# Two-layer decoder on one core: the last mixture's dense pair of groups is routed inside the second layer's attentions, its expert chunks begin at the mixture's second step, and the first set's scatters go three to a step

## The chip, the cores and the metric

The kernel runs on one core of a Trainium2 chip. The metric is the device time of one execution in microseconds (us); lower is better. Everything is float32. PE is the matmul engine (PEld its weight loads), DVE the vector engine, ACT the scalar engine, POOL the general engine that also issues the indirect DMAs, and SP the engine that issues most other DMAs.

## The reference, cut to what matters

The input is 32 sequences of 128 tokens with 128 features each (4096 tokens), and a context of the same shape. Two layers follow each other. Each has self-attention, cross-attention to the context and a mixture of 16 experts of which every token takes 4. The change is about the second layer's mixture:

```
def _swiglu(x, wg, wd, wu):
    return silu(x @ wg.T) * (x @ wu.T) @ wd.T
...
E = 16
TOP_K = 4
```

A router (a 16 x 128 weight and a bias per expert) scores each token against the 16 experts. The four best are taken, a softmax over their four scores gives their weights, and the output of the token is the weighted sum of the four experts' `_swiglu` plus one shared expert's, added to the token. The tokens are normalised ahead of each part (`_layernorm`).

## The kernel before, in words

**Groups, batches, sets.** A group `g` is 512 tokens (`GT`; 8 groups), a batch is 128 tokens (`S`; 4 batches to a group, `GB`; 32 in all, counted by `u`). A set `n` is two groups, so 8 batches (`NBR`); there are 4 sets. In the last mixture the sets 0, 2 and 3 (`SETS`) go by rows, and set 1 (groups 2 and 3) goes dense.

**By rows.** `Tables.route` (L1997) picks the four experts of each token, `Tables.placed` works out a place for each of the 4 x 1024 rows so that the rows of one expert lie together in tiles of 128 rows, and `Tables.way_out` (L2093) sends the normalised rows to these places in DRAM (`rows_in`) with indirect DMAs from POOL: for each batch `u` four of them, one for each choice `k`, 64 KB each, so 32 for a set. A set has 48 tiles, which are worked in 12 quads of four. `rows_of` (L2152) fetches a quad's rows (256 KB, L2154) and, for each tile, reads its expert from `owners` (L2159) and fetches that expert's weights (192 KB, L2162). `rows_turned` (L2170) transposes the rows (`prows`), `rows_up` and `rows_down` make the expert's matmuls (`pg`, `pu`, `pyrows`) and store the result to `rows_out` (L2193). `way_back` (L2198) gathers with 32 indirect DMAs a set, and `added` (L2209) adds the rows times their weights (`parts`) to `x`.

**Dense.** Groups 2 and 3 go through all 16 experts and the shared one, a chunk each: 17 chunks a group, 34 in all. `chunk_up` (L2212) multiplies (`pg<-hx`, `pu<-hx`) and scales the product by the expert's share (L2223), `chunk_down` accumulates into `y`. The shares are made by `route_softmax` (L1771); `send` (L1841) transposes them (`pct`, L1849) and writes them to DRAM (`combined`, L1853), and `fetched` (L2135) reads them back spread over 128 partitions, 1 MB for four experts of a group, four such a group. The shared expert alone is also needed for the other six groups (`alone`, one chunk each).

**The order of the work.** `steps` (L1188) writes the program step by step: in step `s` each stage `(stage, at, every, n)` that is due issues its instructions in the order of the list, and after each of them one piece of the stages under `between` is issued; what is left of these follows at the end of the step. Within `tc.manual_schedule` each named engine keeps exactly this order. The attentions of the second layer (`second_layers`, L2523) are one such run of steps (PE, DVE, ACT and POOL from step 8 on); the last mixture (`last_layer`, L2108) is the next, with SP's order written out too. The step numbers of the two are separate; below they are called attention steps and steps.

**What is routed where.** In the attentions, `rnorm`, `rscaled`, `rturn`, `routing`, `choose`, `placed` and `way_out` prepare set 0, whose scatters go four to an attention step from 35 on. Inside the last mixture, at its own steps, the dense set 1 is normalised (0), scaled (1), turned and routed (2), its shares chosen (3) and sent (4); set 2 is turned and routed at 4, placed at 6 and scattered from 7 on, two batches to a step; set 3 at 10, 12 and 13, one batch to a step. Quad `q` (0 to 35, set by set) is fetched at step `q` - 1 and transposed at step `q` + 1, so set 2's first quad at step 13, and set 3's at step 25. The dense chunks begin at step 6, one a step up to 23, then one every second step up to 36, and two a step after the quads. Set 3's gathers and additions come one batch a step from steps 39 and 41.

Of the kernel before, what the change touches and what calls it, by code (L numbers as in the profile page):

```python
# [9 lines left out]
F32 = mybir.dt.float32  # L10
# [945 lines left out]
def fast_decoder(ctx: ExitStack, tc: tile.TileContext, ins, spans, out: bass.AP):  # L956
# [847 lines left out]
    def mixture(tag, W, route, per, last, weights_of, kept=lambda g: None):  # L1804
# [13 lines left out]
        def turn(wk, g):  # L1818
            pool = edge if g in groups(0) else wk
            hs[g] = pool.tile([128, GT], F32, name="hx", bufs=2 if g in groups(0) else 5)  # L1820
            by_feature(xn.pop(g), hs[g])

        def routing(wk, n):
            lg = sm([128, NBR, E], "logits")
            for i, g in enumerate(groups(n)):
                for b in range(GB):
                    mm(lg[:, i * GB + b, :], lhsT=hs[g][:, bass.ts(b, S)], rhs=W["r"], start=True, stop=True)
            choices[n] = route(lg, edge)
            choose(n, 1)
# [130 lines left out]
    class Tables:  # L1960
# [32 lines left out]
        def kept(self, g):  # L1993
            self.xn[g] = self.spare[:, g]
            return self.xn[g]
# [97 lines left out]
        def way_out(self, n, u):  # L2093
            b, g = u % GB, n * NBR // GB + u // GB
            for k in range(4):
                sent = nc.gpsimd.indirect_dma_start(  # L2096
                    out=rows_in[n],
                    out_offset=bass.IndirectOffsetOnAxis(ap=self.places[n][:, k, u : u + 1], axis=0),
                    in_=self.xn[g][:, b],
                    in_offset=None,  # L2100
                )

                tc.declare_no_dep(sent.ins, group=f"rows{n}", reason="rows of different places")
                tc.add_to_no_dep_group(f"rows{n}", sent.ins)
                nc.gpsimd.nop()
                yield

    def last_layer(tag, W, stages, of_expert, tables):  # L2108
# [3 lines left out]
        send, made = stages[5], stages[-1]  # L2112
# [8 lines left out]
        def scaled(g):  # L2121
            xn[g] = wk.tile([128, GB, D], F32, name="xr", bufs=6)
            yield from normed(wk, g, *factors.pop(g), xn[g], nc.vector)

        def turn(g):
            hs[g] = wk.tile([128, GT], F32, name="hx", bufs=NG - 2)
# [11 lines left out]
        def routing(n):  # L2138
# [4 lines left out]
            choices[n] = tables.route(lg, n) if n in SETS else route_softmax(lg, edge)  # L2143
            next(choices[n])

        def chosen(n):
            comb = yield from choices.pop(n)
            if comb is not None:
                made["combs"][n] = comb
# [96 lines left out]
        for s in range(6, NQ + 1):  # L2246
            if s < 2 * QUADS or s % 2 == 0:
# [7 lines left out]
        at[s + 3], at[s + 5] = alone[4:5], alone[5:6]  # L2255
        LAST = s + 6
# [3 lines left out]
        for before, g in zip([None, *dense_groups], dense_groups):  # L2260
            for j in range(E // NS):
                fetches.append(((g, j), 5 if before is None else step_of[before, NS * j + NS - 1] + 1))
# [19 lines left out]
        def several(stage, keys):  # L2282
            def run(_):
# [5 lines left out]
        dense_n = ({1, 2, 3} - set(SETS)).pop()  # L2289
        n2, n3 = SETS[1:]  # L2290
        batches = lambda n: [(n, u) for u in range(NBR)]
        once = lambda stage, k, s: (lambda _: stage(k), s, 1, 1)
# [4 lines left out]
            (several(turn, of_set(dense_n)), 2, 1, 1),  # L2297
            once(routing, dense_n, 2),
            (lambda _: send(wk, dense_n), 4, 1, 1),
            (several(turn, of_set(n2)), 4, 1, 1),  # L2300
            once(routing, n2, 4),
            once(tables.owned, n2, 8),
            (several(turn, of_set(n3)), 10, 1, 1),
            once(routing, n3, 10),
            once(tables.owned, n3, 14),
# [7 lines left out]
                once(several(norm, of_set(dense_n)), None, 0),  # L2313
                once(several(scaled, of_set(dense_n)), None, 1),
                once(several(norm, of_set(n2)), None, 1),
                once(several(scaled, of_set(n2)), None, 2),
                once(chosen, dense_n, 3),
                once(chosen, n2, 5),
                once(several(norm, of_set(n3)), None, 5),
                once(tables.placed, n2, 6),  # L2320
                *((each(tables.way_out, batches(n2)[i::2]), 7, 1, 4) for i in range(2)),
                once(several(scaled, of_set(n3)), None, 8),
                once(chosen, n3, 11),
                once(tables.placed, n3, 12),
                (each(tables.way_out, batches(n3)), 13, 1, NBR),
# [4 lines left out]
                (each(way_back, batches(n3)), NQ + 3, 1, NBR),  # L2330
                (each(added, batches(n3)), NQ + 5, 1, NBR),
# [191 lines left out]
    def second_layers(stages, early, late, after, tables):  # L2523
# [11 lines left out]
        placed = lambda _: tables.placed(0)  # L2535

# [13 lines left out]
            (first(rturn), 20, 4, R),  # L2550
# [6 lines left out]
            (first(routing), 25, 1, 1),  # L2557
            (lambda _: tables.owned(0), 36, 1, 1),
            between=[
# [4 lines left out]
                (first(rscaled), 19, 4, R, xturn),  # L2564
                (first(rnorm), 18, 4, R),
# [3 lines left out]
                (lambda u: tables.way_out(0, u), 35, 1, NBR),  # L2569
# [39 lines left out]
    mixture0 = mixture("l0f", W0F, route_groups, 2, False, lambda c: (W0F[k][:, bass.ts(c, 128)] for k in "gud"))  # L2609
# [4 lines left out]
    with tc.tile_pool(name="l1early", bufs=1, reuse_waits="tile") as early:  # L2614
# [18 lines left out]
        mixture1 = mixture("l1f", W1F, lambda lg, _: tables.route(lg, 0), 1, True, of_expert, tables.kept)  # L2633
# [39 lines left out]
```

## Time and profile before

| | us |
|---|---|
| median of 6 runs | 1428.47 (1422.72 to 1433.62) |
| the profiled execution's own time | 1429.33 |
| its span, first to last instruction | 1427.5 |
| PE busy | 1270.2 (89%) |
| DVE busy | 856.9 (60%) |
| ACT busy | 576.9 (40%) |
| POOL busy | 533.7 (37%) |
| last mixture, 1128 to 1427: PE busy | 258.59 |
| last mixture: POOL busy | 161.47 |

The span lies 1.83 us below the profiled execution's own time; the rest lies around it. Busy shares are averages over very different stretches, so they say little about a change in one place. A line of a timeline begins with its start and its length in us, then engine, line of the kernel, operation, output and inputs; in brackets is how long the engine stood idle ahead of it, and what ended that. "issue" there means that nothing in the profile ended it. Lines with SPq, ACTq or POOLq are DMA issues.

### The profile page before, as it was taken

Reading aid. Unit: us, or ns where it says so; the run is one execution under the profiler, and the core shown is the slowest. Engines: PE = TensorE matmul, PEld = TensorE weight load, DVE = VectorE, ACT = ScalarE, POOL = GpSimd, SP = SyncE. Lnnn points to the kernel's source line nnn. Section 1 sums busy time; section 2 is a strip of 40 time slices with the busy share of each in tenths; the row PEclk is TensorE's granted clock in tenths of the full one; section 3 lists DMA queues with packets and bytes.
Section 4 is the critical chain, followed back from the end, with each engine's and each line's share of the span. In section 5 each row is a group of like instructions: output and inputs, shape, how many; then the busy total and the mean of one; then the engine's idle time right before and its main releaser. Section 6 shows DMA issues by size and latency. Waiting matters only on the chain. (4 is left out here: it accounts for less than half of the span.)

```text
span 1427.5 us, 27808 instructions
## 1 busy us (share of the span) xinstructions
PE 1270.2 (89%) x10753; PEld 848.1 (59%) x10753; DVE 856.9 (60%) x2271; ACT 576.9 (40%) x848; POOL 533.7 (37%) x729
## 2 busy tenths in 40 slices
PE   3689999999999998699999988999986779789897
PEld 2357777777777786444444455556653476567654
DVE  6646767676776684375775546756664455434564
ACT  1355445454554432223232235545534443234322
POOL 5233242535232140222000115445427416574665
PEclk7789999999999999789999999989988889999999
DMA  9501111111111112525135020000001379599943
GB/s 347 173 1 31 31 31 43 40 41 31 31 32 31 31 39 54 130 46 120 40 80 120 0 95 2 2 1 2 2 4 34 100 230 312 183 305 297 285 142 95
DMA packets 89531, 129.08 MB, mean 90 GB/s; under 512 B 9872, under 2 KB 63760, under 8 KB 87984
## 3 DMA queue, kind: packets, MB, share of 16 engines
q1 hardware_dynamic: 76624, 102.59, 25.9%
q0 software_dynamic: 6144, 12.60, 2.9%
q10 hardware_dynamic: 6624, 12.05, 2.2%
q8 instruction: 87, 1.43, 0.4%
q14 instruction: 52, 0.43, 0.1%
HBM read 99.34 MB, written 27.85 MB: 89 GB/s over the span
## 5 line engine op out<-in xcount | busy, mean ns | idle before, releaser
L1280 ACT ACTIVATE e<-scores 128x1024 f32<-128x1024 f32 x128 | 124.0, 1021 | 64.6 <-PE scores L977 64.6
L977 PE MATMUL y<-sg,wide 128*128 128x512 f32 x224 | 117.6, 613 | 7.4 <-DVE sg L2223 2.5
L977 PE MATMUL pg<-hx,wide 128*128 128x512 f32 x224 | 119.5, 616 | 0.0
L977 PE MATMUL pu<-hx,wide 128*128 128x512 f32 x224 | 118.3, 610 | 0.0
L2198 POOL DMA_INDIRECT back<-rows_out,place x96 | 92.7, 966 | 50.7 <-DVE x L2209 24.6
L1295 DVE STREAM_TRANSPOSE by_token<-sums 128x512 f32<-128x512 f32 x64 | 45.6, 713 | 101.1 <-PE sums L977 101.1
L1126 POOL TENSOR_SCALAR xn<-x,mv,r 128x128 f32<-128x128 f32 x80 | 67.5, 850 | 91.7 <-PE pxn L1135 82.8
L1097 POOL TENSOR_SCALAR r<-mv 128x4 f32<-128x4 f32 x48 | 11.5, 240 | 221.9 <-DVE mv L1116 221.5
L1531 ACT ACTIVATE e<-xscores 128x1024 f32<-128x1024 f32 x64 | 62.0, 1021 | 79.9 <-PE xscores L977 79.9
L1882 ACT ACTIVATE sg<-pg 128x512 f32<-128x512 f32 x72 | 43.0, 597 | 123.0 <-PE pg L977 115.5
L977 PE MATMUL sums<-e,v 128*32 128x128 f32 x2048 | 78.2, 297 | 16.0 <-POOL v L1075 15.4
L977 PE MATMUL scores<-qb,k 32*128 32x512 f32 x512 | 80.8, 703 | 12.9 <-ACT qb L1466 4.5
L1883 DVE TENSOR_TENSOR sg<-sg,pu 128x512 f32<-128x512 f32 x72 | 49.3, 685 | 66.6 <-PE pu L977 63.6
L977 PEld LDWEIGHTS sums<-e,v 128*32 128x32 f32 x2048 | 57.9, 118 | 47.7 <-POOL v L1075 20.8
L1097 POOL TENSOR_SCALAR r2x<-mv 128x2 f32<-128x2 f32 x16 | 3.7, 233 | 210.8 <-DVE mv L1116 210.8
L977 PEld LDWEIGHTS pu<-hx,wide 128*128 128x128 f32 x224 | 43.7, 197 | 54.2 <-issue 51.4
L2096 POOL DMA_INDIRECT rows_in<-xr,place x64 | 62.5, 976 | 34.6 <-issue 18.3
L1579 ACT COPY av<-po 128x512 f32<-128x512 f32 x64 | 37.5, 586 | 89.5 <-PE po L977 89.4
L1545 DVE COPY v<-pval 128x512 f32<-128x512 f32 x64 | 43.5, 680 | 50.1 <-PE pval L977 50.1
L977 PE MATMUL po<-e,v 128*64 128x128 f32 x1024 | 65.3, 280 | 8.5 <-DVE v L1545 8.5
L2183 DVE TENSOR_TENSOR sgrows<-sgrows,pu 128x512 f32<-128x512 f32 x36 | 24.7, 687 | 78.4 <-PE pu L977 48.3
L977 PE MATMUL po<-av,wide 128*128 128x256 f32 x256 | 63.4, 403 | 8.1 <-DVE av L1599 8.1
(300 smaller groups left out, 2920.9 us busy)
## 6 DMA issues: line engine op xcount, KB each, us to landing
row_weights<-in_w1f_dram SPq DMA_DIRECT2D x144, 192.0 KB, 3.7
factor<-factors SPq DMA_DIRECT2D x64, 256.0 KB, 4.7
share<-combined SPq DMA_DIRECT2D x32, 512.0 KB, 11.8
rows_in<-in_few SPq DMA_DIRECT2D x36, 256.0 KB, 4.2
rows<-rows_in SPq DMA_DIRECT2D x36, 256.0 KB, 4.8
rows_out<-yrows ACTq DMA_DIRECT2D x36, 256.0 KB, 3.9
share<-combined SPq DMA_DIRECT2D x8, 1024.0 KB
wide<-in_w1f_dram SPq DMA_DIRECT2D x1, 3272.0 KB
```

Source lines behind the costliest of these rows:

```text
L977: last[0] = nc.tensor.matmul(*args, **kw)
L1126: eng.tensor_scalar(n[:, b, :], x[g][:, b, :], mv[:, b, 0:1], r[:, b : b + 1], ALU.subtract, ALU.mult)
L1280: nc.scalar.activation(e[-1], ps[:, bass.ts(n, 2)].rearrange("p c i s -> p (c i) s"), AF.Exp, scale=scale)
L1295: nc.vector.transpose(tt.rearrange("p i t r -> p (i t r)"), po.rearrange("p i s -> p (i s)"))
L1531: nc.scalar.activation(e[-1], ps[:, n].rearrange("p r c s -> p (r c) s"), AF.Exp, scale=scale)
L1545: nc.vector.tensor_copy(v[:, bass.ts(n, XC), :], pv)
L1579: nc.scalar.copy(avs[w][n][:, :, bass.ts(b, S)], po)
L1882: nc.scalar.activation(sg, pg, AF.Silu)
L1883: nc.vector.tensor_tensor(sg, sg, pu, ALU.mult)
L2096: sent = nc.gpsimd.indirect_dma_start(out=rows_in[n], out_offset=bass.IndirectOffsetOnAxis(ap=self.places[n][:, k, u : u + 1], axis=0), in ...
L2183: nc.vector.tensor_tensor(sg, sg, pu, ALU.mult)
L2198: nc.gpsimd.indirect_dma_start(out=outs[n, u][:, k], out_offset=None, in_=rows_out[n], in_offset=bass.IndirectOffsetOnAxis(ap=places[n][:, ...
```

## The change

The dense set's norm, scaling, turn, routing, choosing and sending move from the mixture's steps 0 to 4 into the attention steps 26 to 43. Its turned groups are kept in the tiles of the context's first two groups (`cx[0]`, `cx[1]`), which the cross-attention has read by then. The share fetches of its first group move from step 5 to step 0. The dense chunks begin at step 1, one a step up to 19, then one every second step up to 36; six of 34 instead of nine are left for the steps after the quads. Set 2's routing moves from step 4 to 2, its placing from 6 to 4 and its scatters from 7 to 5; set 3's from 10, 12 and 13 to 6, 8 and 10. Set 0's scatters go three instead of four to an attention step, over 11 steps instead of 8, from the same step on. Set 3's gathers and additions go two batches a step, and the last step of all is 45 instead of 48. Two rings become shorter (`xr` 6 to 4 tiles, `hx` 6 to 4).

```diff
     def turn(wk, g):
-        pool = edge if g in groups(0) else wk
-        hs[g] = pool.tile([128, GT], F32, name="hx", bufs=2 if g in groups(0) else 5)
+        pool, bufs = (edge, 2) if g in groups(0) else (wk, 5)
+        hs[g] = more[g] if g in more else pool.tile([128, GT], F32, name="hx", bufs=bufs)
         by_feature(xn.pop(g), hs[g])
...
     def kept(self, g):
-        self.xn[g] = self.spare[:, g]
-        return self.xn[g]
+        if g * GB // NBR in SETS:
+            self.xn[g] = self.spare[:, g]
+        return self.xn.get(g)
...
-    def way_out(self, n, u):
-        b, g = u % GB, n * NBR // GB + u // GB
-        for k in range(4):
+    def way_out(self, n, some):
+        for u, k in some:
+            b, g = u % GB, n * NBR // GB + u // GB
...
-        for s in range(6, NQ + 1):
-            if s < 2 * QUADS or s % 2 == 0:
+        for s in range(1, NQ + 1):
+            if s < 20 or s % 2 == 0:
                 at[s] = [todo.pop(0)]
...
-        at[s + 3], at[s + 5] = alone[4:5], alone[5:6]
-        LAST = s + 6
+        at[s + 3], at[s + 4] = alone[4:5], alone[5:6]
+        LAST = s + 5
...
-                fetches.append(((g, j), 5 if before is None else step_of[before, NS * j + NS - 1] + 1))
+                fetches.append(((g, j), 0 if before is None else step_of[before, NS * j + NS - 1] + 1))
...
-            (several(turn, of_set(dense_n)), 2, 1, 1),
-            once(routing, dense_n, 2),
-            (lambda _: send(wk, dense_n), 4, 1, 1),
-            (several(turn, of_set(n2)), 4, 1, 1),
-            once(routing, n2, 4),
-            once(tables.owned, n2, 8),
-            (several(turn, of_set(n3)), 10, 1, 1),
-            once(routing, n3, 10),
-            once(tables.owned, n3, 14),
+            (several(turn, of_set(n2)), 2, 1, 1),
+            once(routing, n2, 2),
+            once(tables.owned, n2, 6),
+            (several(turn, of_set(n3)), 6, 1, 1),
+            once(routing, n3, 6),
+            once(tables.owned, n3, 12),
...
-                once(several(norm, of_set(dense_n)), None, 0),
-                once(several(scaled, of_set(dense_n)), None, 1),
-                once(several(norm, of_set(n2)), None, 1),
-                once(several(scaled, of_set(n2)), None, 2),
-                once(chosen, dense_n, 3),
-                once(chosen, n2, 5),
-                once(several(norm, of_set(n3)), None, 5),
-                once(tables.placed, n2, 6),
-                *((each(tables.way_out, batches(n2)[i::2]), 7, 1, 4) for i in range(2)),
-                once(several(scaled, of_set(n3)), None, 8),
-                once(chosen, n3, 11),
-                once(tables.placed, n3, 12),
-                (each(tables.way_out, batches(n3)), 13, 1, NBR),
+                once(several(norm, of_set(n2)), None, 0),
+                once(several(scaled, of_set(n2)), None, 1),
+                once(chosen, n2, 3),
+                once(several(norm, of_set(n3)), None, 3),
+                once(tables.placed, n2, 4),
+                (each(tables.way_out, to_send(n2, 2)), 5, 1, 4),
+                once(several(scaled, of_set(n3)), None, 5),
+                once(chosen, n3, 7),
+                once(tables.placed, n3, 8),
+                (each(tables.way_out, to_send(n3, 1)), 10, 1, NBR),
...
-                (each(way_back, batches(n3)), NQ + 3, 1, NBR),
-                (each(added, batches(n3)), NQ + 5, 1, NBR),
+                *((each(way_back, batches(n3)[i::2]), NQ + 3, 1, NBR // 2) for i in range(2)),
+                *((each(added, batches(n3)[i::2]), NQ + 5, 1, NBR // 2) for i in range(2)),
...
-            (first(rturn), 20, 4, R),
+            (first(rturn), 20, 4, 2 * R),
...
-            (first(routing), 25, 1, 1),
+            (first(routing), (25, 33), 1, 2),
             (lambda _: tables.owned(0), 36, 1, 1),
+            (lambda _: send(early, 1), 43, 1, 1),
...
-                (first(rscaled), 19, 4, R, xturn),
-                (first(rnorm), 18, 4, R),
+                (first(rscaled), 19, 4, 2 * R, xturn),
+                (first(rnorm), 18, 4, 2 * R),
...
-                (lambda u: tables.way_out(0, u), 35, 1, NBR),
+                (lambda i: tables.way_out(0, to_send[3 * i : 3 * i + 3]), 35, 1, 11),
+                (lambda _: choose(1, 3), 34, 1, 7),
...
-        mixture1 = mixture("l1f", W1F, lambda lg, _: tables.route(lg, 0), 1, True, of_expert, tables.kept)
+        route = lambda lg, n: tables.route(lg, n) if n in SETS else route_softmax(lg, edge)
+        mixture1 = mixture("l1f", W1F, route, 1, True, of_expert, {2: cx[0], 3: cx[1]}, tables.kept)
```

## The prediction

> **What bounds the kernel now.** I read the page's busy shares and chain first: PE is busy 89% of the span, so waits matter only where PE really stops. A table by stretches (columns: length, then busy us of PE, PEld, DVE, ACT, POOL, then clock, DMA share, GB/s) shows where:
>
> ```profile
> 1085.00:1100.00 15.00, 4.38 (x60) 2.98 (x60) 6.37 (x29) 2.41 (x3) 10.70 (x16) 0.75 0.10 32
> 1100.00:1128.00 28.00, 19.15 (x236) 9.61 (x230) 8.55 (x21) 13.16 (x16) 20.86 (x27) 0.80 0.12 39
> 1150.00:1172.00 22.00, 17.21 (x105) 16.16 (x105) 7.76 (x33) 8.69 (x15) 0.00 (x0) 0.77 0.60 181
> 1220.00:1230.00 10.00, 3.23 (x14) 1.92 (x13) 1.45 (x4) 1.18 (x2) 3.35 (x4) 0.79 0.33 90
> 1250.00:1275.00 25.00, 23.16 (x136) 16.68 (x136) 8.32 (x12) 9.26 (x16) 18.90 (x21) 1.00 0.95 308
> 1375.00:1400.00 25.00, 25.00 (x66) 11.61 (x65) 17.46 (x35) 5.96 (x10) 17.91 (x18) 1.00 0.20 61
> ```
>
> The granted clock falls with it. PE is starved at the end of the attentions (1085 to 1128), once near 1150 and once near 1225. After that it is full, but in the middle so is the DMA. The timelines of SP, POOL, PE and ACT then give the chain through the last mixture:
>
> ```profile
> 1124.68 0.96 POOL L2096 DMA_INDIRECT rows_in<-wide,place  x1 [0.30 <-issue]
> 1126.96 0.34 SPq L2154 DMA_DIRECT2D rows<-rows_in  x1
> 1131.87 0.66 PE L2170 MATMUL prows<-in_few,rows 128*128 128x128 f32 x4 [0.85 <-DVE x L1173]
> 1152.83 1.03 PE L1849 MATMUL pct<-in_few,comb 128*16 128x128 f32 x8 [3.94 <-DVE comb L1800]
> 1183.28 1.12 POOL L2096 DMA_INDIRECT rows_in<-xr,place  x1 [5.91 <-DVE expert_ends L2082]
> 1223.31 0.96 POOL L2096 DMA_INDIRECT rows_in<-xr,place  x1 [0.30 <-issue]
> 1225.56 0.33 SPq L2154 DMA_DIRECT2D rows<-rows_in  x1
> 1228.21 1.09 PE L2170 MATMUL prows<-in_few,rows 128*128 128x128 f32 x4 [6.77 <-DMA rows<-rows_in]
> 1298.60 0.33 SPq L2154 DMA_DIRECT2D rows<-rows_in  x1
> 1361.09 0.43 SPq L2154 DMA_DIRECT2D rows<-rows_in  x1
> 1374.00 0.33 ACTq L2193 DMA_DIRECT2D rows_out<-yrows  x1
> 1376.90 0.94 POOL L2198 DMA_INDIRECT back<-rows_out,place  x1 [3.83 <-DVE x L2209]
> 1417.00 0.94 POOL L2198 DMA_INDIRECT back<-rows_out,place  x1 [0.30 <-issue]
> ```
>
> Set 0's last scatter releases the first rows 1.3 us later; step 1 begins at 1131.87. At step 4 PE waits for the dense set's routing (1152.83). Set 2's scatters run back to back, 1183.28 to 1224.27, and PE waits 6.77 us for them at step 13. From 1298.60 to 1361.09 SP fetches 11 quads at 5.68 us each (four weight issues of together 4.3 us, the rest rows and register loads), while a step costs PE 3.11 us, or 5.69 with a chunk: SP and the DMA set the pace there. The last quad's store (1374.00) frees set 3's 32 gathers, 1376.90 to 1417.94, and they set the end.
>
> **The change, part by part.** All sums go against the profiled execution: span 1427.5, time 1429.33, which is 0.86 above the median 1428.47. I follow four marks: first rows fetch F (1126.96), step 13 (1228.21), step 36 (1365.73), end (1427.5).
>
> *Up to F: +11.5.* Three scatters a step take 11 attention steps (35 to 45) instead of 8 (35 to 42). A scatter costs POOL 1.265 us with its gap. At the end of step 39, 15 instead of 20 are out. The stall around 1087 to 1098 contains four scatters between the norm's power and the scaling; one leaves it, so all after it comes 1.27 us sooner: the range check of 1108.58 at 1107.3. From there POOL has 17 scatters (21.5), four copies of v (0.46 with gap, 1.8) and two range checks (3.0): 26.3 us, ending at 1133.6 instead of 1125.64, +8. The second check also waits for the last average, and the scatters of steps 44 and 45 stand behind it. The copies of v come sooner, so attention itself ends about 4 us earlier, but it isn't last any more.
>
> To it come the dense set's norm, turn and routing inside attention steps 26 to 40: two turns on PE (0.66 each), 16 logits (1.85), transposes for the shares (1.03), eight pairs of statistics on DVE (0.46 each), scaling (0.34 on DVE, 0.85 on POOL, four each), some 20 small routing operations (3.9 in all where they stand now). PE has between 8.4 and 10 of every 10 us busy from 985 to 1055, so the turns aren't hidden; the logits fall before the 4.1 us in which PE waits for DVE near 1055, which covers them (1.85 if that cover is gone). I take +3, between +1.3 (turns alone) and +9 (every operation in a row); nothing is removed there, so no gain. Scatters landing beside the share traffic: +0.5, at most +3.
>
> Moved past SP's queue: four share fetches of 1 MB now stand at step 0, ahead of the first rows. They wait for the combined weights sent at attention step 43, landed about 1126 plus 3, so they are issued near 1129 to 1131; 1172 to 1186, where the same fetches ran before, moved about 400 GB/s, so 4 MB take 10.5 us, done about 1141, as the rows are issued at 1138.5. Queued behind them are the rows, then all weights; PE's transposes wait for these. I charge the 2 us overlap to the next mark's slack. The Trainium skill, DMA: Bandwidth & Descriptors, Queues, rings and completion order, says each engine consumes one issuer's descriptors in ring order; it speaks against this placement, and with it the rows could not pass the shares. By the rule 2 us more, by the rows above none if the traffic is thinned by SP's own pace.
>
> *F to step 13: 101.25 to 90.75, −10.5.* The dense routing leaves steps 2 to 4, set 2's takes its place; chunks lie in steps 1 to 12 (12 instead of 7). Each step by its nearest row: F to step 2 was 9.9 (landing, transposes, weights), plus 0.86 for the chunk's down product, 10.8; step 2 (two turns, logits, chunk) like the old step 10, 8.9; step 3 5.7; step 4 with the places like the old step 12, 9.3; step 5 with their DVE chain like the old step 7, 7.4; step 6 for set 3 again 8.9; 5.8; step 8 9.3; 7.4; three of 5.75. Sum 90.75. Set 2's scatters start 2.6 before step 6, as they did before step 8: F+39.5; 32 take 41.0: F+80.5; rows 1.3 and 2.5 later, F+84.3, 6.4 us before PE wants them. So the 6.77 us wait goes, and behind it PE itself is late next. Each us of delay beyond 6.4 in that DVE chain costs a us; bounds −3 and −16.
>
> The idle before step 1 grows to some 11 us, and matmuls after a gap are slow: after the 6.77 us wait, the pair for pg took 1.91 instead of 1.02. But step 1 was slow before too (its eight pg matmuls at 1133.24 took 2.11 where later ones take 1.06), so I add 0. The Trainium skill, TensorE: Matmul & The Clock Gate, What's actually happening, has the clock halved after about 3.4 us idle and back after 3.4 us of work; by it the ceiling would be 1.7 us.
>
> *Step 13 to step 36: 137.5 to 125.3, −12.2.* Set 2's rows leave SP at F+81.8; 23 more quads at 5.6 us (5.36 over the first five, 5.68 late; nearer to the late one, as half of these steps hold a chunk and gathers run) are 128.8, two share issues 0.8, and 4.64 from last fetch to transposes: F+216. PE has 16 instead of 18 chunks here (5.2 us less), so it is not last. Bounds −5 (the chunks alone) and −18 (5.36).
>
> *Step 36 to end: +2.5.* PE's tail loses three chunks (9 to 6, 7.7 us), which buys nothing: the 41.0 us of gathers after the last store remain, and in the old profile both ended within 1 us of each other. Set 3's last additions now stand in step 44, before the last shared chunk (step 45) on DVE, so its multiply (0.70), down product (1.0) and part of the x transposes follow the last gather, +2.5; 0 if DVE were free, +4 with a cold clock.
>
> Sum +11.5 − 10.5 − 12.2 + 2.5 = −8.7: 1429.33 becomes 1420.6, less 0.86 for the median: 1419.8, say 1420.
>
> **The rivals.** *Start hardly later (0.22): 1411.* Added attention work falls into waits (POOL idles 6.1 us between 1068 and 1126, PE 10.6 between 1085 and 1100) and F moves by 3 instead of 11.5. Against it: POOL's sum above.
>
> *Pace unchanged (0.15): 1427.* At 0.95 DMA share a better order moves no more bytes; step 13 to 36 then saves only the two chunks. For it: 308 GB/s between 1250 and 1275. Against it: PE waits for rows there (2.87 and 1.98 us) with cold steps behind them, which the lead of 6.4 us at step 13 removes.
>
> *Shares first (0.10): 1437, slower.* The share buffers may lie where the attentions still work; then the head of SP's queue waits for their end and holds rows and weights back. With the upper bound of the added work the attentions end at 1141 (1131.8 + 9); four issues 1.6, 4 MB at the 286 GB/s of 1330 to 1350 14.7, rows 2.5: step 1 at 1160 instead of 1143, 17 us more. The chunks would be queued from step 1 on but wait there for their shares: the change would not do what it says. It decides if step 1's transposes start after 1158.
>
> **How the numbers follow.** The forecast has 0.53; its own range is 1412 to 1429. 0.5% is 7.1 us, about what a measurement of this kernel can tell from no change; the line is at 1421.3, so the forecast gives 0.30 to faster and 0.23 to no change. With the first rival faster has 0.52, with the second same has 0.38, slower 0.10. The range, 1406 to 1433, reaches into the first rival and past the second, and leaves out most of the third.
>
> **What would show it.** First rows fetch at 1138 (right if 1134 to 1142), the last set-0 scatter near 1136, no PE wait for comb in step 4, no wait above 2 us at step 13, set 2's scatters starting 40 us after the first rows, last store 8 to 14 us earlier, gathers still last. Wrong if rows come before 1131 (faster) or step 1 begins after 1158.

## The result, and the profile after

The changed kernel takes 1431.20 us (median of 37 executions, 1422.46 to 1446.43) and the kernel before, run beside it, 1423.92 (median of 79). The ratio is 1.0062, with a 95% interval of 1.0045 to 1.0078: slower by 0.6%, where I had forecast faster by 0.6%. The profiled execution has a span of 1433.5 us and an own time of 1435.66; the prediction's sum for it was 1420.6.

Four of the stretches that the prediction showed, in the profile after (same columns):

```profile
1085.00:1100.00 15.00, 6.91 (x99) 4.25 (x97) 11.38 (x44) 5.20 (x7) 7.83 (x12) 0.90 0.08 24
1100.00:1128.00 28.00, 19.78 (x223) 10.15 (x223) 8.55 (x21) 13.30 (x16) 22.45 (x29) 0.81 0.12 36
1150.00:1172.00 22.00, 20.41 (x132) 16.05 (x131) 11.86 (x37) 7.92 (x14) 0.00 (x0) 0.97 0.75 218
1220.00:1230.00 10.00, 9.46 (x50) 6.49 (x51) 3.53 (x6) 3.55 (x6) 7.56 (x9) 1.00 0.70 211
```

The two holes that the change was to fill are filled: PE has 20.41 of 22 us around 1160 (17.21 before) and 9.46 of 10 around 1225 (3.23). The timelines of POOL, SP and PE show what was paid for it:

```profile
1128.81 0.78 SPq L1854 DMA_DIRECT2D combined<-xn  x2
1131.77 1.97 SPq L2137 DMA_DIRECT2D share<-combined  x4
1137.28 0.95 POOL L2098 DMA_INDIRECT rows_in<-wide,place  x1 [0.30 <-issue]
1142.60 0.32 SPq L2154 DMA_DIRECT2D rows<-rows_in  x1
1146.05 1.09 PE L2170 MATMUL prows<-in_few,rows 128*128 128x128 f32 x4 [14.33 <-DMA rows<-rows_in]
1183.50 1.09 POOL L2098 DMA_INDIRECT rows_in<-xr,place  x1 [6.17 <-DVE expert_ends L2084]
1238.70 0.60 PE L2170 MATMUL prows<-in_few,rows 128*128 128x128 f32 x4
1376.49 0.33 ACTq L2193 DMA_DIRECT2D rows_out<-yrows  x1
```

PE stands idle for 14.33 us before step 1, which begins at 1146.05 instead of 1131.87. Step 13 (1238.70) no longer waits for set 2's rows. But the last store, at 1376.49, is 2.5 us later than before, not 8 to 14 earlier.

To compare executions I use marks that every kernel has. A, B and C are POOL's range checks of the attentions' results (the first instruction of each, `in_range<-rec`), counted from the end: the sixth, the fourth and the last, 980.07, 1042.90 and 1129.90 in the profile before. (One expectation below counts A and B differently; its times say which are meant.) s1, s13 and s36 are the first transposes of steps 1, 13 and 36. Of each kernel, the us between marks, on a chip of the kind on which the first result was measured:

```
                          A-B     B-C    C-s1   s1-s13  s13-s36  s36-end   A-end
before                  62.83   87.00    1.97   96.34   137.52    61.77   447.43
changed                 71.22   81.15   15.45   92.65   129.52    65.28   455.27
e10_four_again          71.22   85.94   14.44   92.12   128.86    63.94   456.52
e6_four_late            70.40   86.12    2.77   93.78   130.91    65.31   449.29
e8_chunks_to_tail       71.21   86.05    2.93   88.13   135.73    76.42   460.47
e20_all_three_third     63.59   87.88    1.90   93.75   131.86    64.60   443.58
e19_best_again          62.00   87.87    2.56  101.32   131.61    60.12   445.48
```

From A to the end the changed kernel is 7.8 us longer than the one before; the ratio of 1.0062 is 8.8 us. What lies before A is left out, since A itself lies up to 11 us apart in these executions, most of it in stretches that the edits hardly touch (last section). Each row is one execution, and executions of one kernel differ by more than the kernels do: e20_all_three_third took 1410.76 to 1435.79 us, with a median of 1427.76, and the one profiled took 1414.75. So the marks say where time goes, and the ratios how much it is. A second execution of the changed kernel (e9_after_again) repeats its row to 0.3 us.

### The profile page after: what moved, and what is told of

Its sections match the earlier page's. It is cut to its first block, busy times and chain, and to the rows that moved or that the text cites. A ratio compares the mean times of both kernels' runs of the same rounds, so it can differ in the third digit from the quotient of the medians.

```text
span 1433.5 us, 27807 instructions
## 1 busy us (share of the span) xinstructions
PE 1265.8 (88%) x10753; PEld 844.7 (59%) x10753; DVE 854.1 (60%) x2267; ACT 574.9 (40%) x846; POOL 539.0 (38%) x733
## 5 line engine op out<-in xcount | busy, mean ns | idle before, releaser
L1126 POOL TENSOR_SCALAR xn<-x,mv,r 128x128 f32<-128x128 f32 x84 | 72.2, 866 | 91.4 <-PE pxn L1135 82.7
L977 PE MATMUL scores<-qb,k 32*128 32x512 f32 x512 | 79.5, 693 | 11.1 <-ACT qb L1466 4.5
L977 PE MATMUL sums<-e,v 128*32 128x128 f32 x2048 | 75.2, 289 | 12.8 <-POOL v L1075 12.1
L977 PE MATMUL pg<-hx,wide 128*128 128x512 f32 x156 | 83.7, 619 | 0.0
L977 PE MATMUL pu<-hx,wide 128*128 128x512 f32 x156 | 81.8, 606 | 0.0
L977 PEld LDWEIGHTS y<-sg,wide 128*128 128x128 f32 x224 | 36.1, 191 | 65.5 <-DVE sg L1886 36.6
L977 PEld LDWEIGHTS xscores<-qk 64*128 64x128 f32 x1024 | 59.6, 188 | 13.8 <-issue 8.3
```

Of the source, the lines that this page charges most:

```text
L977: last[0] = nc.tensor.matmul(*args, **kw)
L1126: eng.tensor_scalar(n[:, b, :], x[g][:, b, :], mv[:, b, 0:1], r[:, b : b + 1], ALU.subtract, ALU.mult)
```

## The experiments

The chips that ran them are of two kinds: on one the kernel before takes about 1424 us, on the other 1543 to 1551. Each ratio is to the kernel before on the same chip. I call them the faster and the slower chip, but that the chip makes the difference isn't shown: of the chip numbers that the runs carry (15, 8, 2 and 11), number 8 stands at runs of both kinds. The expectations call PE TensorE, DVE VectorE, ACT ScalarE and POOL GpSimd.

**1. The spread alone, and without it.** My first theory was a late start made by the spread (as the prediction had it); the rivals were the early chunks and the shares' transfer. e1_four and e10_four_again are the same kernel on the slower and the faster chip, e2_three_only and e14_three_again another one, both on the slower.

```diff
 # e1_four, e10_four_again: the changed kernel with
-                (lambda i: tables.way_out(0, to_send[3 * i : 3 * i + 3]), 35, 1, 11),
+                (lambda i: tables.way_out(0, to_send[4 * i : 4 * i + 4]), 35, 1, NBR),
 # e2_three_only, e14_three_again: the kernel before with
-                (lambda u: tables.way_out(0, u), 35, 1, NBR),
+                (lambda i: tables.some_out(0, to_send[3 * i : 3 * i + 3]), 35, 1, 11),
```

> The changed kernel with one thing undone: the first set's 32 scatters go four to an attention step in 8 steps again (everything else as changed). Late-start theory (the changed kernel starts its last mixture 15.6 us later and the later stages win back only about 10): the first scatter stays at about 1075, the last ends 57.6 us after it as it does before the change, at about 1132 instead of 1138.2, the first row fetch comes at about 1136 instead of 1142.6, and the run is 5 to 7 us faster than the changed kernel, level with the kernel before or a few us under it (ratio to before 0.997 to 1.002). Rival, early chunks (the loss is made behind the row fetch, in steps 4, 8 and 9, where VectorE's placing chain holds the chunks): the fetch comes earlier, but the steps stretch, and the time stays within 2 us of the changed kernel's (ratio 1.005 to 1.008). Rival, shares (the 4 MB of weights ahead of the rows delay the scatters' landing): landing to fetch stays at 4 us or grows to 5 or more, and 2 to 4 us at most are won (ratio 1.002 to 1.005).

> The kernel before with only the spread: the first set's scatters three to a step in 11 attention steps. Late-start theory: the first scatter stays at 1068, the last ends 6 to 8 us later than in the kernel before (about 1132 to 1134 instead of 1125.6), the first row fetch follows 1.3 us behind it, and most of it reaches the end: 4 to 8 us slower (ratio 1.003 to 1.006). Rivals (early chunks, or shares): the spread itself is harmless, as the stall of step 13 and the late dense chunks absorb it: within 2 us of before (ratio 0.999 to 1.0015).

> The changed kernel with the first set's scatters four to a step in 8 steps. Late-start theory: last scatter at about 1132 (57.6 us after the first at about 1075) instead of 1138; but SP's queue now holds the first row fetch behind the four share fetches (issued 1131.8 to 1133.7 in the changed kernel), so the fetch comes at 1135 to 1136.5 instead of 1142.6 and the run is 4 to 7 us faster than the changed kernel. Rival, early chunks: within 2 us of the changed kernel.

> The kernel before with only the spread, three scatters to a step in 11 steps, on a chip of the faster kind. Here no share stands in front of the rows, so the last scatter sets step 1: last scatter 6 to 8 us later than before (about 1132 to 1133), step 1 at about 1138, and 4 to 7 us of it reach the end, as the waits at step 4 and step 13 move along with it: ratio 1.003 to 1.005. Rival (the spread is harmless): 1.000 within 0.0015.

e1_four: 1.0042 (1.0003 to 1.0081). e10_four_again: 1.0092 (1.0058 to 1.0126), where the changed kernel had 1.0056 (1.0019 to 1.0092) on the same chip. On the slower chip the changed kernel had 1.0038 (e15_after_third, below). So undoing the spread gained nothing, and the theory fell that the spread makes the loss here. The timelines of SP and PE in e10_four_again show why:

```profile
1132.68 2.02 SPq L2137 DMA_DIRECT2D share<-combined  x4
1134.80 0.39 SPq L2154 DMA_DIRECT2D rows<-rows_in  x1
1145.98 1.09 PE L2170 MATMUL prows<-in_few,rows 128*128 128x128 f32 x4 [13.33 <-DMA rows<-rows_in]
```

The last scatter is issued at 1127.42 here, 10 us earlier than in the changed kernel, and the rows are fetched 7.8 us earlier. Yet step 1 starts at 1145.98, as late as with the spread: the 256 KB of rows take 11.2 us from issue to transposes, behind 4 MB of shares. From the first share's issue to step 1 the DMA share is 0.93 at 367 GB/s here, and 0.91 at 346 in the changed kernel: in both some 4.9 MB move while PE waits. In the changed kernel the spread cost nothing; from B to s1 it even saved 3.8 us (96.60 against 100.38), since the attentions end sooner, as the prediction had said of the spread (B-C is 81.15 against 85.94), and the combined factors are sent behind them.

Alone the spread does cost what the prediction had charged: e2_three_only has 1.0057 (1.0015 to 1.0098) and e14_three_again 1.0078 (1.0042 to 1.0115). In both step 1 comes 11.7 to 11.8 us after C, where e4_dense_in_attn below, also without shares in front but four to a step, has 1.97. The rival by which the spread is harmless holds only where the shares stand in front.

**2. The shares behind the rows.** e3_share_late and e13_late_again are one kernel (slower chip); e6_four_late also has four scatters to a step (faster chip). e9_after_again is the changed kernel beside the latter.

```diff
-                fetches.append(((g, j), 0 if before is None else step_of[before, NS * j + NS - 1] + 1))
+                fetches.append(((g, j), 1 + j if before is None else step_of[before, NS * j + NS - 1] + 1))
-        for s in range(1, NQ + 1):
-            if s < 20 or s % 2 == 0:
+        for s in range(3, NQ + 1):
+            if s < 24 or s % 2 == 0:
```

> The changed kernel with the first dense group's four weight shares fetched one a step at steps 1 to 4, behind the first two row fetches in SP's queue, and its chunks from step 3 on (one a step to step 23, then every second). Shares theory: the first row fetch follows the last scatter by 1.3 us again instead of 4.4, the whole mixture moves forward by 3 us and the time falls by 3 us or more (ratio to before about 1.004 or less). Late-start theory: landing improves by up to 3 us, but two chunks move from the cheap first steps behind the rows, so 1 to 3 us are won (ratio 1.004 to 1.006). Early chunks theory: steps 4, 8 and 9 stay at 11, 11 and 9 us, and less than 1 us changes (ratio 1.005 to 1.007).

> The changed kernel with only the shares behind the rows (scatters still three to a step); its sister ran on the slower chip. Shares theory: in the changed kernel the 4 MB of shares are what holds step 1 (it began 15.5 us after the attentions' end with three and with four scatters to a step). With the shares out of the way the last scatter (1137) decides: first row fetch at about 1139, step 1 at 1142 to 1143 instead of 1146; 1 to 4 us faster than the changed kernel, and 3 to 6 us slower than e6_four_late, which has four to a step. If the spread cost nothing at all it would be level with e6_four_late.

> The changed kernel with both: four scatters to a step, and the first group's share fetches one a step at steps 1 to 4 behind the rows, its chunks from step 3 on. Late-start theory: the first row fetch follows the last scatter by 1.3 us, at about 1133.5, 9 us earlier than in the changed kernel; 6 to 9 us faster than it, ratio to before 0.997 to 1.002. Shares theory: 3 us or more faster than e10_four_again. Early chunks theory: within 2 us of the changed kernel.

> The changed kernel once more, beside the next three on one chip. The four runs so far were on a chip where the kernel before takes 1551 us instead of 1424. Late-start theory: ratio to before about 1.006 if the chip is like the first one; on a chip like the second one 1.005 to 1.012, with the last scatter 6 us or more behind that of e1_four.

e3_share_late 1.0033 (0.9993 to 1.0072) and e13_late_again 1.0076 (1.0045 to 1.0107): with three scatters to a step the last of them sets step 1 instead, 11.8 and 11.9 us after C, and little is won. e6_four_late: 1.0038 (1.0005 to 1.0071). The ratio alone doesn't separate it from the changed kernel (1.0056). The marks do:

```profile
1125.31 1.37 SPq L2154 DMA_DIRECT2D rows<-rows_in  x1
1129.00 1.09 PE L2170 MATMUL prows<-in_few,rows 128*128 128x128 f32 x4 [1.65 <-DVE xr L1126]
1136.81 0.43 SPq L2137 DMA_DIRECT2D share<-combined  x1
```

Step 1 follows C by 2.77 us instead of 15.45, and the wait before it is for DVE, no longer for rows. From B to s1 the kernel is as fast as the one before (88.89 against 88.97). Between s1 and s13, where the shares now are, it takes 1.1 us more than the changed kernel. With this 1.9 us of the 7.8 remain from A to the end: 7.6 lost in A-B, 5.7 won behind it.

**3. Chunks out of the early steps.** Steps 4, 6, 8 and 9 took 11.0, 9.8, 11.4 and 8.6 us in the changed kernel, together 5.8 more than I had written for them.

```diff
 # e8_chunks_to_tail: e6_four_late with
-            if s < 24 or s % 2 == 0:
+            if s not in (4, 6, 8, 9) and (s < 24 or s % 2 == 0):
```

> e6_four_late with four chunks taken out of steps 4, 6, 8 and 9 (which took 11.0, 9.8, 11.4 and 8.6 us in the changed kernel, where later steps take 5.7) and put behind the last rows, where TensorE is idle 15 of the last 33 us beside the gathers. Early chunks theory: each of the four steps is 2 to 3 us shorter, the last row store comes 8 to 12 us earlier than in e6_four_late, and so does the end (ratio to e6_four_late 0.992 to 0.995). Late-start theory alone (behind the row fetch SP's pace of 5.7 us a quad sets the time): the steps get shorter but SP takes the time back, and less than 3 us is won.

1.0088 (1.0054 to 1.0121): 7 us slower than e6_four_late, which both theories had wrong. s1-s13 did become 5.7 us shorter, but s13-s36 4.8 longer, and the tail 11.1 longer. The windows of s13-s36 show what holds that stretch, in the kernel before, the changed one and this one:

```profile
1228.21:1365.73 137.52, 125.03 (x756) 93.93 (x757) 59.85 (x124) 51.69 (x88) 87.17 (x91) 0.97 0.91 290
```
```profile
1238.70:1368.22 129.52, 118.42 (x745) 91.40 (x743) 52.31 (x105) 50.15 (x85) 77.11 (x81) 0.99 0.91 285
```
```profile
1222.75:1358.48 135.73, 122.29 (x756) 92.86 (x757) 54.75 (x107) 51.21 (x87) 79.17 (x84) 1.00 0.91 287
```

All three run at a DMA share of 0.91 and 285 to 290 GB/s, and PE is busy 0.90 to 0.91 of each, so shares don't tell them apart. SP's row fetches do. These are the first of set 2 and the last of set 3, in the changed kernel and then in this one; the kernel before has them at 1225.56 and 1361.09:

```profile
1228.63 0.37 SPq L2154 DMA_DIRECT2D rows<-rows_in  x1
1363.81 0.43 SPq L2154 DMA_DIRECT2D rows<-rows_in  x1
```
```profile
1217.65 0.33 SPq L2154 DMA_DIRECT2D rows<-rows_in  x1
1354.23 0.43 SPq L2154 DMA_DIRECT2D rows<-rows_in  x1
```

The 23 quads between them take 135.5 us before, 135.2 in the changed kernel and 136.6 here: 5.9 a quad, and 134.5 to 136.9 in all seven kernels of the table. What differs is how far the first fetch lies ahead of step 13: 2.65 us before, 10.07 in the changed kernel, 9.59 in e6_four_late, 5.10 here. So the 8 us that the changed kernel gains between s13 and s36 are the wait for set 2's rows turned into lead, and no faster pace. In e8_chunks_to_tail PE comes to step 13 sooner, but the fetch waits 4.9 us for set 2's last scatter, so 4.5 us of the lead are gone, and what the shorter early steps gained with them. The four chunks then stand behind the last gather: the end comes 22.9 us after it. What sets the 5.9 us, SP's own issues or the DMA at 0.91, no run here separates.

**4. The dense routing in the attentions, and its place there.** e4_dense_in_attn is the kernel before with only the dense pair's norm, scaling, turn, routing and sending moved into the attentions. e11_shift and e16_shift_again are the changed kernel with the dense pair's norm, scaling and turns two attention steps later. e15_after_third is the changed kernel beside e16. All ran on the slower chip.

```diff
 # e11_shift, e16_shift_again: the changed kernel with
-            (first(rturn), 20, 4, 2 * R),
+            (first(rturn), (20, 24, 30), 4, 2 * R),
-            (first(routing), (25, 33), 1, 2),
+            (first(routing), (25, 35), 1, 2),
-                (first(rscaled), 19, 4, 2 * R, xturn),
-                (first(rnorm), 18, 4, 2 * R),
+                (first(rscaled), (19, 23, 29), 4, 2 * R, xturn),
+                (first(rnorm), (18, 22, 28), 4, 2 * R),
-                (lambda _: choose(1, 3), 34, 1, 7),
+                (lambda _: choose(1, 3), 36, 1, 7),
```

> The kernel before with only the routing of the dense pair moved: its scaling, turning, gates, top-k and the sending of its factors lie in the attentions; scatters four to a step, the chunks still from step 6, the shares at step 5, the second and third sets at their old steps. Late-start theory: the first scatter comes 6 to 7 us later (about 1074.5) and the last at about 1132; against that the 10 us stall of TensorE at step 4 (waiting for the combined factors) is gone: the time is within 3 us of before, either way (ratio 0.998 to 1.002). Early chunks theory (routing early is good, only the early chunks and the early placing lose): clearly faster than before by 5 us or more (ratio 0.996 or less). Shares theory: the scatters land in 1.3 us here, since no share is in the queue, and the run is 3 us or more under e1_four.

> The changed kernel with the dense pair's statistics, scaling and turns two attention steps later (28 to 34 instead of 26 to 32, its routing from 35 instead of 33), where no other group's norm stands in the same step. Theory now, queue: 8.4 us are lost between the attentions' third-last and fifth-last range checks (980 to 1043), since TensorE waits 2.2 and 3.4 us for the cross attention's scaled rows, queued on GpSimd and VectorE behind the dense pair's statistics. Then these two waits go, the stretch loses about 3 us instead of 8.4, and the run is 3 to 6 us faster than the changed kernel: ratio to before 1.002 to 1.004. Rival, work: the 8.4 us are TensorE's and the queues' added work wherever it stands: within 1.5 us of the changed kernel (1.005 to 1.007).

> The changed kernel beside the next three, as their base. On a chip of the faster kind 1.0056 to 1.0062 as before; on the slower kind it has not been measured: 1.004 to 1.009.

> The changed kernel with the dense pair's norm, scaling and turns two attention steps later, and nothing else. Queue theory: 980 to 1043 loses nothing or 1 us instead of 8.4, so the first scatter comes 6 to 9 us earlier; but step 1 still starts behind the shares, which wait for the combined factors, sent two steps' worth later in the order but at the same attention step 43: 3 to 7 us faster than the changed kernel (ratio to it 0.995 to 0.998). Work theory: within 1.5 us of it.

In every kernel with the routing in the attentions and without the shift, A-B is 70.4 to 72.1 us (e4: 71.24); in e2 and e14, which have it in the mixture, 62.86 and 62.87. The waits of PE in the changed kernel between 978 and 1050 name the place; the kernel before has no such lines there:

```profile
PE pxn L1135 <- POOL xn L1126: 4.1, 4, 2.6
PE pxn L1135 <- DVE xn L1126: 1.6, 2, 1.1
```

5.7 us of the 8.4: the turn of the cross attention's scaled rows waits. POOL's timeline of the changed kernel at the second place, and the same place in e20_all_three_third, which has the shift:

```profile
1030.01 1.04 POOL L1098 TENSOR_TENSOR r<-r,half 128x4 f32<-128x4 f32 x1
1033.46 0.23 POOL L1097 TENSOR_SCALAR r<-mv 128x4 f32<-128x4 f32 x1 [2.42 <-DVE mv L1116]
1033.77 1.05 POOL L1098 TENSOR_TENSOR r<-r,half 128x4 f32<-128x4 f32 x1
1034.83 2.87 POOL L1126 TENSOR_SCALAR xn<-x,mv,r 128x128 f32<-128x128 f32 x2
```
```profile
1018.11 1.04 POOL L1098 TENSOR_TENSOR r<-r,half 128x4 f32<-128x4 f32 x1
1019.25 1.58 POOL L1126 TENSOR_SCALAR xn<-x,mv,r 128x128 f32<-128x128 f32 x2
```

The cross attention's factors are ready at 1031.05. The next instruction in POOL's order is the dense pair's power, and POOL stands 2.42 us until DVE has that pair's statistics; only then come the scaled rows PE waits for. With the shift the scaling follows at once. A-B falls to 62.01 (e11) and 63.59 (e16), 8.5 us less than the 72.07 of e15, so the work theory fell. The times are 1.0014 (0.9974 to 1.0053) and 1.0015 (0.9984 to 1.0046), and e15's 1.0038 (1.0005 to 1.0072): in the expected direction, inside the intervals. Part of it is given back in B-C (96.78 against 93.91), and step 1 still waits for the shares (15.26 after C). e4_dense_in_attn has 1.0017 (0.998 to 1.0053), as the late-start theory said.

**5. All together, and the old tail.** e12, e17 (slower chip) and e20 (faster) are one kernel: e6_four_late with the shift. e18 (slower) and e19 (faster) also have the tail of the kernel before.

```diff
 # e18_shift_tail, e19_best_again: besides
-        at[s + 3], at[s + 4] = alone[4:5], alone[5:6]
-        LAST = s + 5
+        at[s + 3], at[s + 5] = alone[4:5], alone[5:6]
+        LAST = s + 6
-                *((each(way_back, batches(n3)[i::2]), NQ + 3, 1, NBR // 2) for i in range(2)),
-                *((each(added, batches(n3)[i::2]), NQ + 5, 1, NBR // 2) for i in range(2)),
+                (each(way_back, batches(n3)), NQ + 3, 1, NBR),
+                (each(added, batches(n3)), NQ + 5, 1, NBR),
```

> e6_four_late (four scatters to a step, shares one a step behind the rows, chunks from step 3) with the dense pair's norm two attention steps later. Queue theory: 3 to 6 us faster than e6_four_late, ratio to before 0.997 to 1.001: level with the kernel before or a little under it. Work theory: as e6_four_late, 1.002 to 1.005.

> Norm shifted, shares behind the rows, four scatters to a step. Queue theory and shares theory together: the attentions lose about 1 us instead of 8.4, step 1 follows the attentions' end as in the kernel before (1.3 to 4 us), and the later gain of 5 to 8 us remains: ratio to before 0.995 to 0.999, 8 to 14 us faster than the changed kernel. If only one of the two terms is real: 1.000 to 1.003.

> As the run before it, with the third set's gathers and additions one batch a step again and the last shared chunk one step later, as in the kernel before. Tail theory (the last additions stand before the last chunk on VectorE and its products run on a cold TensorE clock): last gather to end 3 us shorter, 1 to 4 us faster than the run before it. Rival (the gathers alone set the end): the same within 1 us.

> All four edits once more. On a chip of the faster kind: e6_four_late stood at 1.0038; the shift takes 5 to 9 us off the attentions, the old tail 2 to 3: ratio 0.993 to 0.999. On the slower kind 0.990 to 0.997 as before.

> The same without the old tail. On a chip of the faster kind 0.996 to 1.001, 2 to 3 us above the run before it, and its stretch between the range checks at 980 and 1043 as long as in the kernel before within 1.5 us; on the slower kind 0.994 to 1.001.

Three edits: 0.9956 (0.9921 to 0.9991) and 0.9977 (0.9941 to 1.0013) on the slower chip, 0.9995 (0.9954 to 1.0037) on the faster. With the old tail: 0.993 (0.9899 to 0.9962) and 0.9967 (0.9929 to 1.0004). So the version with all four is faster than both kernels on the slower chip; on the faster one it is faster than the changed kernel (1.0056 to 1.0062), and against the kernel before its interval just reaches 1. e20 shows both mended terms at once, A-B 63.59 and C-s1 1.90, and is 11.7 us shorter than the changed kernel from A on; by the ratios some 9 us.

The tail: in the changed kernel the last additions of DVE stand before the last chunk's multiply, and two products follow on a cold clock:

```profile
1418.85 0.95 POOL L2198 DMA_INDIRECT back<-rows_out,place  x1 [0.30 <-issue]
1421.38 0.35 DVE L2209 SCALAR_TENSOR_TENSOR x<-back,parts,x 128x128 f32<-128x128 f32 x1 [0.72 <-DMA back<-rows_out,place]
1422.38 2.07 PE L977 MATMUL y<-sg,wide 128*128 128x512 f32 x2 [3.66 <-DVE sg L2221]
1424.25 1.91 PE L977 MATMUL y<-in_few,x 128*128 128x128 f32 x8
1426.19 0.59 ACT L2236 COPY y<-y 128x512 f32<-128x512 f32 x1 [7.70 <-PE y L977]
```

From the end of the last gather to the end are 13.7 us, before 9.6, in e19 8.0. In time the tail's worth isn't settled: e18 is below e17 by 0.0047 and e19 below e20 by 0.0028, both within the intervals. e19's profile lost more in s1-s13 (101.32 against e20's 93.75) than its tail won: steps 5 and 6 took 9.38 and 14.17 us instead of 5.72 and 9.98, and from 1150 to 1180 the granted clock was 0.80, in e20 1.00 from 1152 to 1180. The order of the work is the same in that stretch, and why the clock fell is open.

## Why the prediction was wrong

The steps of the sum, predicted and measured, profile against profile:

```
                       predicted   measured
up to F                  +11.5      +15.6
F to step 13             -10.5       -5.2
step 13 to step 36       -12.2       -8.0
step 36 to end            +2.5       +3.5
sum                       -8.7       +6.0
```

The sum was off by 14.7 us: 4.1 up to F, 9.6 from F to step 36, 1.0 behind it. Up to F the miss is really larger, since the profile after comes to A 1.8 us sooner than the one before, in a stretch that the change hardly touches.

**Up to F: the size was near, the causes were not.** "I take +3" for the dense pair's work in the attentions is the first step that failed: 8.4 us are lost from A to B, and 1.0 to 1.2 of them come back up to the next range check in the changed kernel and e10. I had counted what the work costs PE and let POOL's and DVE's operations lie beside it. I did not ask who stands behind them in these two queues: the cross attention's scaling. My own upper bound, 9, was the case "every operation in a row". Placed where no other norm is due, the same work costs 0.8 us in A-B and 0.9 in B-C (e20).

"I charge the 2 us overlap to the next mark's slack" is the second. The shares ahead of the rows did not cost 2 us or none, but set step 1: with them behind, C-s1 is 2.77 instead of 15.45. In e10_four_again rows issued 0.1 us behind the last share took 11.2 us. I had even named the rule against it, that each engine consumes one issuer's descriptors in ring order (the Trainium skill, DMA: Bandwidth & Descriptors, Queues, rings and completion order), and this agrees with it. Whether the order in the ring or the shared bandwidth does it, no run here separates. And the estimate of 10.5 us for 4 MB was near (step 1 comes 14.3 us after the first share's issue with the spread, 13.3 without); it was set against a rows fetch that the spread had put late, and so its own weight was hidden.

"+8" for the spread was the right price for the spread alone (C-s1 of 11.7 against 2.0, less 2 for the attentions' earlier end), but not here, where the shares end later anyway. And from the end of the last scatter to the first fetch it took 4.4 us instead of 1.3, beside the shares' traffic: 3.1 more, where I had taken 0.5 and at most 3.

**F to step 13, and step 13 to 36: right in kind, too large by 5.3 and 4.2.** Both waits went as forecast: none for `comb` in step 4, none for rows at step 13, and set 2's scatters start 40.9 us after F (39.5 in the text). Two terms were mis-sized. Steps 4, 6, 8 and 9 were each longer than the old steps I had taken as rows, 5.8 us together; up to step 13 `y` waits 4.9 us for DVE's share multiply, 2.1 before. And "23 more quads at 5.6 us" fails: with their two shares they take 135.2 us instead of 129.6, and they leave SP at F+86.0 instead of F+81.8. The old profile had the right pace. I had read 5.36 over the first five, but its sixth fetch comes here:

```profile
1254.66 0.50 SPq L2154 DMA_DIRECT2D rows<-rows_in  x1
```

That is 5.82 each (5.62 up to the fifth fetch), and over all 23 it is 5.89, as after the change (5.88). So the rival "pace unchanged", which I had weighted at 0.15, was right about the pace. It had the gain of this stretch as two chunks, 5.2 us; 8.0 came, as lead. Mending the start doesn't mend these: e20 gains 10.3 us from F to step 36, where the sum has 22.7.

**Step 36 to end: right mechanism,** +3.5 within its bounds; the cold clock, which I had left out of the value taken, makes two products 1.9 us longer and covers the difference: after 3.66 us idle the granted clock is 0.50 from 1422 to 1427, and the pair for y took 2.07 us, warm ones in this tail 1.02. The Trainium skill, TensorE: Matmul & The Clock Gate, What's actually happening, has the clock halved after about 3.4 us idle, and the trace agrees.

**"Shares first", the slower rival, came true in a milder form.** It was priced at 17 us by waiting buffers, with step 1 after 1158 as its sign. Step 1 began at 1146.05, and the queue's head waited for no buffer. What decided was the place behind 4 MB.

## What to carry to other kernels

Work that moves into a full stretch is priced by the queue it joins, not by its own length: look up, on each engine that keeps the written order, which instruction stands behind it and who waits for that one. A large transfer ahead of the first small one set the start of the whole stage here, whatever else was made earlier; it belongs behind the first fetches. A pace is read over the whole stretch to which it is applied, not over its two ends. And where two costs meet at one mark, undo them together: here each of the two alone (four scatters, or late shares with three) won nothing that could be measured.

## What the runs showed of the hardware that I had not expected

The two kinds of chip are alike where POOL issues no indirect DMA: the same kernel has A-B at 71.22 us on both (e1_four and e10_four_again). Behind B it is longer on the slower one in every stretch that has such DMAs, most of all from s1 to s13 (162.57 against 92.12), where PE and SP stand still while POOL scatters sets 2 and 3. SP's timeline and the window in e4_dense_in_attn:

```profile
1201.56 18.37 SPq L2163 DMA_DIRECT2D row_weights<-in_w1f_dram  x4
```
```profile
1210.00:1230.00 20.00, 0.00 (x0) 0.00 (x0) 0.00 (x0) 0.60 (x1) 15.13 (x17) 0.57 0.30 89
```

Four weight issues take 18.37 us, PE does nothing for 20 us, and the DMA share is only 0.30. On the faster chip four such issues take 4 to 6 us beside the same scatters. The cause is open.

A stretch that the edits hardly touch, from the eighth-last range check to A, took 74.1 us in the kernel before, 71.3 in the changed one in two executions, and 68.0 to 68.4 in e6, e10, e19 and e20. The granted clock goes with it: over this stretch 0.88 in the kernel before, 0.93 in the changed one and 0.97 in e10, with PE busy 66.30, 63.30 and 60.22 us for the same work. Such steps of 3 us are over a third of what this case turned on, and a reason to compare from a mark and not by spans.
